# Moving a pair's weighted rows one slot later on VectorE, between the next pair's two small weight operations, in a two-layer graph attention kernel

## The chip, the cores and the metric

The kernel runs on one core of a Trainium2 chip (trn2). The time is device microseconds (us) from start to end of one execution on that core. The kernel before takes 2144.38 us, the median of three runs (2143.71 to 2145.70).

## The reference

6250 nodes with 768 features are normalised and rectified, sent through two graph attention layers (4 heads of 64, then 1 head of 256) and two dense layers, and added to the input. There are 100000 edges, sorted by destination, and a self loop for each node. What bears on the change is the attention layer:

```python
def gat_conv(x, src, dst, W, a_src, a_dst, bias, heads):
    h = (x @ W).reshape(n, heads, -1)
    alpha_s = (h * a_src[None]).sum(-1)
    alpha_d = (h * a_dst[None]).sum(-1)
    e = leaky_relu(alpha_s[src] + alpha_d[dst], 0.2)
    e = exp(e - segment_max(e, dst)[dst])
    alpha = e / (segment_sum(e, dst)[dst] + 1e-16)
    out = segment_sum(h[src] * alpha[:, :, None], dst)
    return out.reshape(n, -1) + bias
...
h = maximum(layernorm(x), 0)
h = relu(gat_conv(h, src, dst, W1, a_src1, a_dst1, b1, 4))
h = relu(gat_conv(h, src, dst, W2, a_src2, a_dst2, b2, 1))
return x + relu(h @ Wm1 + bm1) @ Wm2 + bm2
```

## The kernel before

**Stages.** First, node features, scores and a table of rows in device memory are made, a tile of 128 nodes at a time. Then `layer_edges` (L530) runs for layer 1 and again for layer 2. Between the edges of a layer, a `Node` object turns finished sums into the next table (layer 1, L778) or into the output (layer 2, L878).

**Tiling.** Edges go in tiles of 128, a *pair* is two tiles, a *group* is two pairs (`TPG = 4`). There are 196 groups; 782 tiles hold edges, so a layer has 391 pairs. The order is written out by hand (`manual_schedule`, L304): each engine works through its own instructions in the order in which the Python code issues them. The loop over groups is at L708.

**One pair.** For every tile, `gather` (L545) issues one indirect DMA from GpSimd (POOL) that fetches 128 table rows into `G` (L554). Then `pair` (L612) does the following:

- ScalarE takes two exponentials of the gathered scores, `e1` (L619) and `e2` (L621).
- VectorE multiplies `v = e2 * rho` (L624) and takes `w = max(v, e1)` (L634 in layer 1, L627 in layer 2). These are the two small weight operations. `rho`, `v`, and in layer 1 also `w`, lie in `e_ps` in PSUM.
- VectorE makes the weighted rows `hw`. In layer 1 this is one multiplication of the gathered rows by `w` (L636); in layer 2 it is two tensor-scalar instructions that write a weighted one-hot matrix from `iota_ps` (L631).
- TensorE adds two products to the sums `o_ps` (L648). Layer 1 multiplies the one-hot tile `hot` (L582) with `hw`; layer 2 multiplies `hw` with `G`.

So the last reader of `G` is VectorE in layer 1 and TensorE in layer 2.

**Around it.** Two pairs stand in each group. Between them come `advance` (steps of the node work), `make_hot(g + 1)`, every fourth group `meet(t + 1)` (16 small matmuls, L600, that spread the destinations' `rho`), and every other group `make_mask`. Behind the second pair come `join` (L608), and in every odd group `gather_up` (L659), which adds up `o_ps` on VectorE (`acc`, L669) and copies parts of it on ScalarE (`sum`, L678). The first tiles of each layer are fetched before the table is complete (L300) and put right in `first_whole` (L275).

**Buffers.** `G` comes from a pool of twenty pairs, which both layers share, and the gathers of group g + 8 stand ahead of pair (g, 0):

```python
gp = ...tile_pool(name="gathered", bufs=2 * (AHEAD + 2))   # AHEAD = 8
...
gather(g + AHEAD)
pair(g, 0)
```

Of the kernel before, what the change touches and what calls it, by code (L numbers as in the profile page):

```python
# [30 lines left out]
NG = NQ  # L31
# [22 lines left out]
def kernel(  # L54
# [21 lines left out]
    nc = tc.nc  # L76
# [440 lines left out]
    def fetch_rows(r):  # L517

        if r < NET // 16:
            drow[r] = rowsp.tile([P, 16 * P], BF16, name="drow")  # L520
            nc.sync.dma_start(drow[r], bcast(dmod_d, 16 * P, r * 16 * P))
# [8 lines left out]
    def layer_edges(layer, H, node, pre, matched, pre_pool):  # L530
# [4 lines left out]
        with tc.tile_pool(name=f"eg{layer}", bufs=5) as eg, \  # L535
                tc.tile_pool(name=f"hw{layer}", bufs=10 if layer == 1 else 14) as hwp, \
                tc.tile_pool(name=f"sum{layer}", bufs=4) as sums, \
                tc.tile_pool(name=f"sm{layer}", bufs=4) as sm:
            G, hot, e_ps, o_ps = {}, {}, {}, {}

            def tiles(g):

                return range(max(TPG * g, FIRST) - TPG * g, min(TPG * g + TPG, LAST) - TPG * g)

            def gather(g):  # L545
                if not 0 <= g < NG:
                    return
                for t in tiles(g):
                    k = TPG * g + t
                    if k // 2 not in G:  # L550
                        G[k // 2] = first_G[layer].get(k // 2) or rows_in(layer)
                    if k < FIRST + len(THERE[layer]):
                        continue
                    nc.gpsimd.indirect_dma_start(  # L554
                        out=G[k // 2][:, k % 2], out_offset=None, in_=table[layer],
                        in_offset=bass.IndirectOffsetOnAxis(ap=src_i[:, k:k + 1], axis=0))
# [18 lines left out]
            def make_hot(g):  # L575

                if layer == 2 or not 0 <= g < NG:
                    return
                T = tiles(g)
                k, n = TPG * g + T[0], len(T)  # L580
                hot[g] = eg.tile([P, TPG, P], F32, name="hot")
                nc.vector.tensor_tensor(  # L582
                    hot[g][:, T[0]:T[0] + n], iota_ps.unsqueeze(1).to_broadcast([P, n, P]),
                    dcol[:, k:k + n].unsqueeze(2).to_broadcast([P, n, P]), ALU.is_equal)
# [27 lines left out]
            def pair(g, p):  # L612

                if 2 * p not in tiles(g):
                    return
                Gp = G.pop(TPG // 2 * g + p)
                sc = Gp[:, :, RW[1]:] if layer == 1 else Gp[:, :, HID:HID + 1]
                e1 = sm.tile([P, 2, H], F32, name="e1")
                nc.scalar.activation(e1, sc, AF.Exp)  # L619
                e2 = sm.tile([P, 2, H], F32, name="e2")  # L620
                nc.scalar.activation(e2, sc, AF.Exp, scale=SLOPE)  # L621
                at = TPG * (g % 4) + 2 * p
                rho, v, w = (e_ps[g // 4][:, at:at + 2, k * H:(k + 1) * H] for k in range(3, 6))
                nc.vector.tensor_mul(v, e2, rho)  # L624
                if layer == 2:
                    w = sm.tile([P, 2, H], F32, name="w")
                    nc.vector.tensor_max(w, v, e1)  # L627
                    hw = hwp.tile([P, 2, P], F32, name="hw")
                    for t in range(2):
                        k = TPG * g + 2 * p + t  # L630
                        nc.vector.tensor_scalar(hw[:, t], iota_ps, dcol[:, k:k + 1], w[:, t],  # L631
                                                ALU.is_equal, ALU.mult)
                else:
                    nc.vector.tensor_max(w, v, e1)  # L634
                    hw = hwp.tile([P, 2, H, C + 1], F32, name="hw")
                    nc.vector.tensor_mul(  # L636
                        hw, Gp[:, :, :RW[1]].rearrange("p t (h c) -> p t h c", h=H),
                        w.unsqueeze(3).to_broadcast([P, 2, H, C + 1]))
                u = g // 2
                if u not in o_ps:  # L640
                    o_ps[u] = ps.tile([P, RW[layer]], F32, name="o_ps", tag="o", bufs=3)
                for t in range(2):
                    k = 2 * p + t
                    if layer == 2:
                        l, r = hw[:, t], Gp[:, t]
                    else:
                        l, r = hot[g][:, k], hw[:, t].rearrange("p h c -> p (h c)")
                    nc.tensor.matmul(o_ps[u], l, r[:, :RW[layer]], start=(g % 2 == 0 and k == 0),  # L648
                                     stop=(g % 2 == 1 and k == tiles(g)[-1]))

            def stay_warm(n):

                if layer == 1:
                    for _ in range(n):
                        nc.tensor.matmul(idle_ps[0], idle[:, :P], idle, start=True, stop=True)
# [3 lines left out]
            def gather_up(u):  # L659

                if u == NU - 1:

                    late.append(node.steps(NT - 1, None, run[0], o_ps.pop(u)))
                    return
                acc = sums.tile([P, RW[layer]], F32, name="acc")
                if u == 0:
                    nc.vector.tensor_copy(acc, o_ps.pop(u))
                else:
                    nc.vector.scalar_tensor_tensor(acc, run[0], keep[:, u % 2:u % 2 + 1],  # L669
                                                   o_ps.pop(u), ALU.mult, ALU.add)  # L670
                for Q in (2 * u - 1, 2 * u):
                    t, q = divmod(Q, 4)
                    if not 0 <= t < NT - 1:
                        continue
                    if q == 0:
                        done[t] = sums.tile([P, RW[layer]], F32, name="sum", bufs=3)
                    r = slice(32 * q, 32 * q + 32)
                    nc.scalar.activation(done[t][r], acc[r], AF.Copy)  # L678
                    if q == 3:
                        late.append(node.steps(t, done.pop(t)))  # L680
                if u == NU - 2:
                    nc.vector.memset(acc[96:], 0.0)
                    run[0] = node.whole(NT - 1, acc)
                else:
                    run[0] = acc

            def advance(g):

                for _ in range(2 if NG - 4 <= g < NG - 2 else 1):
                    for step in list(late):  # L690
                        if next(step, 0) == 0:
                            late.remove(step)
# [15 lines left out]
            for g in range(NG):  # L708
                t, j = divmod(g, 4)
                if g == NG - 2:  # L710
                    at_end.append(g)
                gather(g + AHEAD)
                pair(g, 0)
                if g == NG - 1:
                    pair(g, 1)
                if g == NG - 2:
                    gather_up(NU - 2)
                advance(g)
                if g <= NG - 4:
                    make_hot(g + 1)  # L720
                if g in (NG - 4, NG - 3):
                    make_hot(g + 2)
                if j == 0:
                    if layer == 1:
                        fetch_rows(t + 4)
                    node.prefetch(t)
                    meet(t + 1)
                elif j == (2 if t < NT - 1 else 1):
                    node.ahead(t)
                elif j % 2:  # L730
                    make_mask((g + 7) // 2)
                if g == NG - 3:
                    idle_ps.append(ps.tile([P, 4 * P], F32, name="idle_ps", tag="e"))
                if g >= NG - 3:
                    stay_warm(3)
                if g < NG - 1:
                    pair(g, 1)
                advance(g)
                if j == 3:
                    join(t + 1)  # L740
                if g % 2 and 5 <= g < NG - 6:
                    gather_up((g - 5) // 2)
                elif g in (NG - 6, NG - 5, NG - 3):
                    gather_up({NG - 6: NU - 5, NG - 5: NU - 4, NG - 3: NU - 3}[g])
                if NG - 3 <= g < NG - 1:
                    stay_warm(3)
                hot.pop(g, None)
                if layer == 1 and g == NG - 6:
                    first_sources(2)
            gather_up(NU - 1)  # L750
# [22 lines left out]
    with tc.tile_pool(name="w2p", bufs=1) as wp, tc.tile_pool(name="wk2", bufs=2) as wk:  # L773
# [48 lines left out]
        with tc.tile_pool(name="pre1", bufs=1) as pre:  # L822
            first_hits(pre, 1, 0)
            pre1 = prepare(pre, 1, 4)
            layer_edges(1, 4, Node1(), pre1,
                        lambda: scores_in(ps, w2, *w2_in, KH, 1), pre)
# [428 lines left out]
```

## Time and profile before

| what | value |
|---|---|
| time, median of 3 runs | 2144.38 us (2143.71 to 2145.70) |
| profiled execution: its own time, its span | 2556.39 us, 2554.4 us |
| mean granted TensorE clock in it | 0.760 |
| busy: PE, DVE, POOL, ACT | 1572.4, 1325.8, 1599.2, 545.2 us |
| gathers L554 on POOL | 1545, 951 ns each |
| v L624, w L634, hw L636 in layer 1 | 391 each; 166, 174, 695 ns |
| v L624, w L627 in layer 2 | 391 each; 157, 159 ns |
| hw L631 in layer 2 | two per pair, 406 ns recorded |

The profiled execution is 412 us longer than the median. Its timeline is therefore read for durations and for distances between instructions in undisturbed stretches, and not for the total of its idle times. In a timeline line the columns are: start in us, length in us, engine, line of the source, operation, output and inputs, count, and in brackets the idle time before it and what ended that. PE is TensorE's matmul, PEld its weight load, DVE VectorE, ACT ScalarE, POOL GpSimd, SP the engine whose queue issues plain DMAs.

### The profile page before, as it was taken

The page shows a single profiled execution, that of the slowest core. Times are in us where ns is not written, and L with a number is a line of the kernel's source. Part 1 is how long each engine was busy: PE and PEld are TensorE (multiplying, and loading weights), DVE is VectorE, ACT ScalarE, POOL GpSimd, SP SyncE. Part 2 cuts the span into 40 slices and gives each one's busy share as a digit, 9 for nine tenths or more (in the row PEclk, how much of TensorE's full clock was granted, in tenths as well). Part 3 has the DMA queues.
Part 4 walks back from the last instruction along what each step waited for, and adds up shares of the span by engine and source line. Part 5 has one row for each costly group of instructions (what it writes and reads, how often), then busy time and mean ns, then how long its engine had stood idle before and what let it go on. Part 6 is the DMA issues. An engine that isn't in the chain of part 4 may idle for free.

```text
span 2554.4 us, 26518 instructions
## 1 busy us (share of the span) xinstructions
PE 1572.4 (62%) x6764; PEld 1116.8 (44%) x6765; DVE 1325.8 (52%) x4164; ACT 545.2 (21%) x2601; POOL 1599.2 (63%) x1759
## 2 busy tenths in 40 slices
PE   9963455545554556546554557666676676666667
PEld 7852334433433334324342444444454444444444
DVE  7844555555655556546562444444444444444444
ACT  4630111111121111112121112222222222222212
POOL 6875666666666666666635566666666666666661
PEclk9986677667777777777776777777877787778789
DMA  9954454445454454444434444544554455445442
GB/s 353 344 164 145 128 148 138 132 138 150 135 147 140 136 149 141 137 136 146 138 91 134 125 134 130 152 149 136 155 151 144 142 153 152 144 144 153 147 150 66
DMA packets 157543, 383.12 MB, mean 150 GB/s; under 512 B 35543, under 2 KB 50222, under 8 KB 157382
## 3 DMA queue, kind: packets, MB, share of 16 engines
q0 software_dynamic: 75072, 209.10, 30.4%
q1 hardware_dynamic: 80940, 170.75, 19.1%
q10 hardware_dynamic: 1370, 1.48, 0.2%
q8 instruction: 58, 0.95, 0.1%
q14 instruction: 103, 0.84, 0.1%
HBM read 323.07 MB, written 58.13 MB: 149 GB/s over the span
## 4 chain that ended last, share of the span: by engine, by line
DVE 18%; another core or an unknown queue 15%; PE 14%; issue 13%; ACT 3%; DMA 0%; POOL 0%; ACTq 0%; DVEq 0%; POOLq 0%
PE o_ps L648 8%; DVE hw L631 6%; DVE hw L636 3%; PE y_ps L939 3%; DVE e_ps L624 2%; DVE w L627 1%; PE tp L923 1%; ACT sum L678 1%; DVE acc L669 1%; DVE y L942 1%; DVE e_ps L634 1%; PE e_ps L600 1%; DVE hot L582 1%; PE y_ps L875 0%
## 5 line engine op out<-in xcount | busy, mean ns | idle before, releaser
L554 POOL DMA_INDIRECT G<-table,src_i x1545 | 1469.0, 951 | 822.9 <-issue 535.8
L648 PE MATMUL o_ps<-hw,hot 128*128 128x260 f32 x1564 | 541.4, 482 | 316.2 <-issue 204.4
L648 PEld LDWEIGHTS o_ps<-hw,hot 128*128 128x128 f32 x1564 | 344.8, 235 | 482.5 <-issue 278.6
L648 PE MATMUL o_ps<-G,hw 128*128 128x258 f32 x1564 | 488.2, 460 | 61.3 <-issue 41.2
L648 PEld LDWEIGHTS o_ps<-G,hw 128*128 128x128 f32 x1564 | 352.8, 233 | 168.7 <-issue 59.6
L624 DVE TENSOR_TENSOR e_ps<-e,e_ps 128x8 f32<-128x8 f32 (+1 forms) x782 | 126.5, 162 | 515.7 <-ACT e L621 172.4
L678 ACT ACTIVATE sum<-acc 32x260 f32<-32x260 f32 (+1 forms) x384 | 159.9, 416 | 991.4 <-DVE acc L669 730.4
L600 PE MATMUL e_ps<-win,mask 128*128 128x12 bf16 (+1 forms) x1564 | 88.2, 169 | 372.7 <-issue 356.5
L636 DVE TENSOR_TENSOR hw<-G,e_ps 128x520 f32<-128x520 f32 x391 | 271.9, 695 | 76.9 <-DVE e_ps L634 46.3
L631 DVE TENSOR_SCALAR hw<-iota_ps,dcol,w 128x128 f32<-128x128 f32 x782 | 285.0, 406 | 17.7 <-DVE w L627 2.9
L600 PEld LDWEIGHTS <-mask 128*128 128x128 bf16 x1564 | 75.2, 103 | 393.5 <-issue 369.3
L942 DVE TENSOR_TENSOR y<-y_ps,xt 128x384 f32<-128x384 f32 (+1 forms) x98 | 54.0, 552 | 233.5 <-remote 209.6
L619 ACT ACTIVATE e<-G 128x8 f32<-128x8 f32 (+1 forms) x782 | 151.4, 195 | 110.5 <-issue 57.7
L939 PE MATMUL y_ps<-wm,mT 128*128 128x384 f32 x392 | 160.9, 535 | 11.1 <-issue 7.5
L582 DVE TENSOR_TENSOR hot<-iota_ps,dcol 128x512 f32<-128x512 f32 x196 | 133.5, 681 | 34.1 <-remote 34.1
L621 ACT ACTIVATE e<-G 128x8 f32<-128x8 f32 (+1 forms) x782 | 149.4, 192 | 0.0
L350 PE MATMUL h_ps<-w,r 128*128 128x256 f32 x588 | 135.0, 384 | 4.4 <-ACT r L341 4.4
L923 PE MATMUL tp<-rT,wm 128*128 128x128 f32 x392 | 68.0, 328 | 111.4 <-issue 81.9
L634 DVE TENSOR_TENSOR e_ps<-e_ps,e 128x8 f32<-128x8 f32 x391 | 68.1, 174 | 131.5 <-remote 96.4
L769 ACT ACTIVATE rT<-tp,bT 128x128 f32<-128x128 f32 x196 | 60.7, 362 | 293.5 <-remote 243.3
L350 PEld LDWEIGHTS h_ps<-w,r 128*128 128x128 f32 x588 | 109.7, 193 | 22.6 <-ACT r L341 5.7
L923 PEld LDWEIGHTS tp<-rT,wm 128*128 128x128 f32 x392 | 59.8, 229 | 125.6 <-issue 91.1
(405 smaller groups left out, 1201.3 us busy)
## 6 DMA issues: line engine op xcount, KB each, us to landing
xt<-in_x SPq DMA_DIRECT2D x96, 384.0 KB
drow<-dmod_d SPq DMA_DIRECT2D x49, 512.0 KB
mask_d<-mask SPq DMA_DIRECT2D x97, 256.0 KB
mask<-mask_d SPq DMA_DIRECT2D x97, 256.0 KB
G<-table,src_i POOLq DMA_INDIRECT x1545
xTt<-in_xT SPq DMA_DIRECT2D x49, 384.0 KB
out<-y SPq DMA_DIRECT2D x48, 384.0 KB
table<-kept SPq DMA_DIRECT2D x49, 132.0 KB
```

The costliest lines, as they stand in the source:

```text
L350: nc.tensor.matmul(h_ps, r[:, k], w1[:, k], start=(k == 0), stop=(k == KI - 1))
L554: nc.gpsimd.indirect_dma_start(out=G[k // 2][:, k % 2], out_offset=None, in_=table[layer], in_offset=bass.IndirectOffsetOnAxis(ap=src_i[:, ...
L582: nc.vector.tensor_tensor(hot[g][:, T[0]:T[0] + n], iota_ps.unsqueeze(1).to_broadcast([P, n, P]), dcol[:, k:k + n].unsqueeze(2).to_broadca ...
L600: nc.tensor.matmul(e_ps[t][:, at + k, :3 * H], m[:, k * P:(k + 1) * P], pre.win[:, 2 * u + 2], start=True, stop=True)
L619: nc.scalar.activation(e1, sc, AF.Exp)
L624: nc.vector.tensor_mul(v, e2, rho)
L631: nc.vector.tensor_scalar(hw[:, t], iota_ps, dcol[:, k:k + 1], w[:, t], ALU.is_equal, ALU.mult)
L636: nc.vector.tensor_mul(hw, Gp[:, :, :RW[1]].rearrange("p t (h c) -> p t h c", h=H), w.unsqueeze(3).to_broadcast([P, 2, H, C + 1]))
L648: nc.tensor.matmul(o_ps[u], l, r[:, :RW[layer]], start=(g % 2 == 0 and k == 0), stop=(g % 2 == 1 and k == tiles(g)[-1]))
L678: nc.scalar.activation(done[t][r], acc[r], AF.Copy)
L923: nc.tensor.matmul(m_ps[:, j], wm1[:, k, j * P:(j + 1) * P], rT[:, k], start=(k == 0), stop=(k == KH - 1))
L939: nc.tensor.matmul(y_ps, mT[:, j], wm2[:, j, s * half:(s + 1) * half], start=False, stop=(j == KH - 1))
```

## The change

In `pair`, what follows the two small operations is split off into `onto_sums`: the `hw` instructions and the two products into `o_ps`. `pair` now issues `v` of its own pair, then `onto_sums` of the pair before, then its own `w`, and leaves its own pair in the list `weighed` for the next call. In the last two groups (`g >= NG - 2`) a pair's `onto_sums` follows at once. Nothing is computed that wasn't, and no buffer count is altered. In the changed kernel `hw` is at L644 (layer 1) and L640 (layer 2), `w` at L629, the products at L656; `v` stays at L624.

```diff
-            G, hot, e_ps, o_ps = {}, {}, {}, {}
+            G, hot, e_ps, o_ps, weighed = {}, {}, {}, {}, []
...
                 nc.vector.tensor_mul(v, e2, rho)
+                while weighed:
+                    onto_sums(*weighed.pop())
                 if layer == 2:
                     w = sm.tile([P, 2, H], F32, name="w")
-                    nc.vector.tensor_max(w, v, e1)
+                nc.vector.tensor_max(w, v, e1)
+                weighed.append((g, p, Gp, w))
+                if g >= NG - 2:
+                    onto_sums(*weighed.pop())
+
+            def onto_sums(g, p, Gp, w):
+
+                if layer == 2:
                     hw = hwp.tile([P, 2, P], F32, name="hw")
                     for t in range(2):
                         k = TPG * g + 2 * p + t
                         nc.vector.tensor_scalar(hw[:, t], iota_ps, dcol[:, k:k + 1], w[:, t],
                                                 ALU.is_equal, ALU.mult)
                 else:
-                    nc.vector.tensor_max(w, v, e1)
                     hw = hwp.tile([P, 2, H, C + 1], F32, name="hw")
                     nc.vector.tensor_mul(
                         hw, Gp[:, :, :RW[1]].rearrange("p t (h c) -> p t h c", h=H),
...
-                hot.pop(g, None)
+                hot.pop(g - 1, None)
```

## The prediction, made before the changed kernel had run

> **What bounds the kernel now.** I read the page's busy shares and cost groups first, then the timeline of GpSimd alone, then all engines in an undisturbed stretch, and last the starts of the two layers.
>
> ```profile
> PE 1572.4 (62%) x6764; PEld 1116.8 (44%) x6765; DVE 1325.8 (52%) x4164; ACT 545.2 (21%) x2601; POOL 1599.2 (63%) x1759
> ...
> L554 POOL DMA_INDIRECT G<-table,src_i x1545 | 1469.0, 951 | 822.9 <-issue 535.8
> ...
> L636 DVE TENSOR_TENSOR hw<-G,e_ps 128x520 f32<-128x520 f32 x391 | 271.9, 695 | 76.9 <-DVE e_ps L634 46.3
> L631 DVE TENSOR_SCALAR hw<-iota_ps,dcol,w 128x128 f32<-128x128 f32 x782 | 285.0, 406 | 17.7 <-DVE w L627 2.9
> ```
>
> No engine is above 63%, so shares do not name the bound. But a gather never follows the last without a gap. In the timeline, around two gathers of layer 1:
>
> ```profile
> 1009.03 0.17 DVE L624 TENSOR_TENSOR e_ps<-e,e_ps 128x8 f32<-128x8 f32 x1
> 1009.24 0.17 DVE L634 TENSOR_TENSOR e_ps<-e_ps,e 128x8 f32<-128x8 f32 x1
> 1009.35 0.95 POOL L554 DMA_INDIRECT G<-table,src_i  x1 [0.30 <-issue]
> 1009.44 0.69 DVE L636 TENSOR_TENSOR hw<-G,e_ps 128x520 f32<-128x520 f32 x1
> 1010.06 0.68 DVE L582 TENSOR_TENSOR hot<-iota_ps,dcol 128x512 f32<-128x512 f32 x1
> 1010.60 0.95 POOL L554 DMA_INDIRECT G<-table,src_i  x1 [0.31 <-issue]
> ```
>
> 0.95 plus 0.30 us: GpSimd takes a gather every 1.25 us when nothing stops it. Now add that up for the unprofiled run. The first early gather (L300) starts at 146.25 and the first L554 of layer 1 at 157.48. 774 gathers of layer 1 x 1.25 = 967.5, which gives 1125.0; layer 2 has 11 + 771 = 782, x 1.25 = 977.5, which gives 2102.5. The median is 2144.4, so 41.9 us remain. Of these 2.0 lie around the span (2556.39 - 2554.4) and 20.7 are the end of layer 2 (last e2, L621, starts at 2533.70; the span ends at 2554.4). That leaves **19.2 us** for the switch between layers, two landings and every stall of GpSimd. The kernel is paced by gathers from end to end. The 412 us that the profiled execution is longer are mostly stalls of its own: GpSimd's last gather of layer 1 starts at 1313.12 in it, where 157.48 + 773 x 1.25 is 1123.7.
>
> The others keep up. `acc` (L669) comes once in two groups; in layer 1 it starts at 1302.28, 1309.88, 1319.09 and 1326.29, so two groups cost 24.0 / 3 = 8.0 us of the slowest engine's time, against 8 x 1.25 = 10.0 for their gathers. In layer 2 neighbouring `acc`s stand 6.9 apart (1720.16, 1727.03).
>
> The exception is the start of a layer, where GpSimd fills its twenty pairs and then waits for pair 0 to let go of its rows:
>
> ```profile
> 196.44 0.95 POOL L554 DMA_INDIRECT G<-table,src_i  x1 [0.30 <-issue]
> 206.37 0.17 DVE L624 TENSOR_TENSOR e_ps<-e,e_ps 128x8 f32<-128x8 f32 x1
> 206.57 0.17 DVE L634 TENSOR_TENSOR e_ps<-e_ps,e 128x8 f32<-128x8 f32 x1
> 206.78 0.69 DVE L636 TENSOR_TENSOR hw<-G,e_ps 128x520 f32<-128x520 f32 x1
> 207.40 0.68 DVE L582 TENSOR_TENSOR hot<-iota_ps,dcol 128x512 f32<-128x512 f32 x1
> 208.00 0.16 DVE L624 TENSOR_TENSOR e_ps<-e,e_ps 128x8 f32<-128x8 f32 x1
> 208.22 0.95 POOL L554 DMA_INDIRECT G<-table,src_i  x1 [10.84 <-issue]
> ...
> 1402.90 0.95 POOL L554 DMA_INDIRECT G<-table,src_i  x1 [0.30 <-issue]
> 1419.31 0.94 POOL L554 DMA_INDIRECT G<-table,src_i  x1 [15.46 <-ACT e L619]
> ```
>
> The reader is to see that the gather at 208.22 follows the end of pair 0's `hw` (207.47). The label "issue" means that no releaser was seen. By the 19.2 us, at most part of these 10.5 and 15.2 us (less the usual 0.30) is in the unprofiled run.
>
> **What the Trainium skill says.** "DMA: Bandwidth & Descriptors", section "SWDGE vs HWDGE vs iDMA": a DMA issued from GpSimd, an indirect one too, has its descriptors computed in software there. The steady 0.95 us of L554 agrees. "SBUF — State Buffer", section "Who interferes with whom": GpSimd is shut out of a port pair that it shares with VectorE while VectorE runs in a two-port mode, and with its reads while a VectorE instruction has two SBUF inputs. Here `hw` takes `e_ps` or `iota_ps` from PSUM, and the gather at 1009.35 keeps its 0.95 us beside L636; the change alters no operand's place, so I take no effect from it. "VectorE: DVE Perf Modes", section "The DRAIN you can't avoid": a semaphore between VectorE operations costs nothing extra. The trace differs for small ones: `v` to the dependent `w` is 0.20 us from start to start, while the copy L155 at 205.84 is followed by the independent L608 after 0.07. I use the trace.
>
> **The change, part by part.**
> *VectorE's order.* Nothing is removed: 391 pairs a layer keep one `v`, one `w` and their `hw`. Before, layer 1 has two dependent steps per pair: 0.21 (`v` to `w`), 0.20 (`w` to `hw`), then 0.62 to what follows: 1.03. After, `v`, `hw` of the pair before, `w`: in layer 1 `hw` still carries a wait on VectorE itself (it reads the PSUM tile that `v` writes), so 0.20; `hw` to `w` 0.62; `w` to an independent successor about 0.08, an estimate from L155's 0.07. Sum 0.90, saving 0.13. In layer 2 before: 0.19 + 0.19 + 0.65 = 1.03; after, `hw` has no such wait: 0.08 + 0.65 + 0.20 (the next `v` waits for `w`) = 0.93, saving 0.10. In all 391 x 0.13 + 391 x 0.10 = **90 us of VectorE time**. From both sides: 0 if every step stays held, 391 x 2 x 2 x 0.12 = 188 if none is. On the path it counts 0, because 8.0 us of work already hide behind 10.0 us of gathers. If that cover were gone, it would be a gain.
> *The wait that `hw` inherits.* It now stands behind `v` of the next pair, which waits for that pair's e2 and so for its gather to land. Behind it on VectorE are `w`, `make_hot`, `acc`; TensorE's products wait for it. In the steady state this is one pair's gathers, 2.5 us, of delay in a pipeline that has twenty pairs: 50 us. `gather_up` at the end of odd group g reads sums whose last pair is of group g - 4, so it waits for nothing new. Cost 0.
> *Release of `G`.* One slot later. It counts only where GpSimd stands at the end of its buffers, that is at pair 0. Layer 1: `hw` of pair 0 moves from 206.78 behind `hot` and `v` of pair 1: 206.78 + 0.62 + 0.20 = 207.60, **+0.8 us**. Layer 2: there is no `hot`; `hw` moves behind one `v`, +0.1 to +0.2, and the products behind `meet(1)`, whose 16 matmuls take 0.54 us (L600 at 1418.40) and can run before `hw` is there: **+0.2**, at most +0.7. If the stall at the start is not in the unprofiled run, each is 0.
> *Ends.* In group NG - 2 VectorE does two `hw` in one slot (+0.7 us), and `acc` of `gather_up(NU - 2)` waits for products issued just ahead of it, about +0.3. Three pairs at 2.5 us each follow, in which VectorE needs 1.03: gone before the last landing. 0, at most +0.8 per layer.
> *Queues.* No DMA is moved. GpSimd's and SP's instructions keep their order; ScalarE's too.
> Sum: 0 + 0 + 0.8 + 0.2 + 0 = +1.0, halved for the chance that the stalls are absent: +0.5. Against the profiled execution's 2556.39 it is the same +0.5, and that execution has stalls that move far more; against the median it gives 2144.9.
>
> **Rivals.**
> *Compute sets part of the pace (faster).* For it: GpSimd waited 129.0 us for ScalarE's L928 and 59.8 for L769 in the profile. Against it: the 19.2 us. That is the ceiling; half of it gives 2144.4 - 9.6 = 2134.8.
> *Late release at a full pool (slower).* If GpSimd meets the end of its buffers more often than at two starts, each meeting costs one slot of layer 1, about 1.7 us (206.37 to 208.00). For it: in the profile it does so often. Against it: the 19.2 us allow few. It decides from the third meeting on (3 x 1.7 = 5.1); five give +8.5, 2152.9. `hw` held behind a `v` that waits for ScalarE adds up to 1.25 us where `sum` (L678) stands ahead of `e1`, which belongs to the same case.
> *The change does not do what it says.* The changed kernel's instruction order has `v`, `hw`, `w` in both layers, so this is excluded.
>
> **How the numbers follow.** What a measurement of this kernel can tell from no change is 0.2%, 4.3 us. No effect on the path: 0.74, at 2144.9, own range 2143 to 2148. Late release: 0.17. Compute pace: 0.09. The range reaches into both, 2137 to 2154, and leaves out the far halves of the two rivals.
>
> **What would show it.** In the changed profile: gathers still 0.95 + 0.30; `v` to `hw` to `w` as 0.2 (layer 1) or 0.08 (layer 2) and 0.62 to 0.65; idle before L629 near zero; pair 0's `hw` one slot later in layer 1. GpSimd stalls more often in undisturbed stretches, or a gather interval other than 1.25, would prove me wrong; so would a time below 2140 or above 2149.

## The result: 6 us slower, and the profile after

The changed kernel takes **2152.34 us** (median of 7 runs, 2147.24 to 2153.69) against 2145.70 us for the kernel before (7 runs beside it, 2143.55 to 2149.14). The ratio is 1.0028 [1.0016, 1.0040], or +6.0 us [3.4, 8.6]. That is slower by more than the 0.2% that was set as the measurable bound. It lies inside the predicted range, but outside the 2143 to 2148 of the likeliest case, and above the 2149 that the prediction had named as a sign of being wrong.

Some chips grant TensorE a mean clock of about 0.76 and run the kernels of this document in 2550 to 2595 us, with or without a profile, others grant 0.82 to 0.84 and run them in 2143 to 2155. The profile before came from the first kind and the profile after from the second, so idle times of the two pages are not compared as an effect of the change; distances between a few instructions are.

The page of the changed kernel, shares of the engines and cost groups (columns as before: busy time, mean ns of one, idle time before it and its main releaser):

```profile
PE 1577.6 (73%) x6762; PEld 1088.8 (51%) x6765; DVE 1263.3 (59%) x4164; ACT 598.4 (28%) x2601; POOL 1603.2 (75%) x1759
...
L554 POOL DMA_INDIRECT G<-table,src_i x1545 | 1472.9, 953 | 470.8 <-issue 256.3
...
L624 DVE TENSOR_TENSOR e_ps<-e,e_ps 128x8 f32<-128x8 f32 (+1 forms) x782 | 129.7, 166 | 789.5 <-ACT e L621 780.0
...
L619 ACT ACTIVATE e<-G 128x8 f32<-128x8 f32 (+1 forms) x782 | 160.3, 205 | 1104.4 <-DMA G<-table,src_i 1066.6
...
L640 DVE TENSOR_SCALAR hw<-iota_ps,dcol,w 128x128 f32<-128x128 f32 x782 | 282.5, 402 | 0.1
L644 DVE TENSOR_TENSOR hw<-G,e_ps 128x520 f32<-128x520 f32 x391 | 271.9, 695 | 12.5 <-DVE e_ps L624 0.9
```

Three things are to be seen. A gather still costs 0.95 us and the two forms of `hw` take as long as before (695 and 402 ns, against 695 and 406). VectorE is 62.5 us less busy than in the page before (1263.3 against 1325.8). And VectorE has time to spare: ahead of `v` (L624) it stands idle 789.5 us, waiting for ScalarE's second exponential, which in turn follows L619, and L619 waits 1066.6 us for landings. In such a stretch a saving on VectorE only makes that wait longer.

GpSimd's own waits (engine, line, releaser: total us, times, longest us) show the pace. The longest waits ahead of L554 are:

```profile
POOL G L554 <- issue: 256.3, 841, 0.4
POOL G L554 <- PE o_ps L656: 54.5, 179, 0.3
```

No wait ahead of an L554 is longer than 0.4 us, from the first to the last. GpSimd never stood at the end of its twenty pairs in this execution.

**The new order, layer 1 and layer 2.** From the timeline of the changed kernel, one pair each:

```profile
1113.86 0.17 DVE L624 TENSOR_TENSOR e_ps<-e,e_ps 128x8 f32<-128x8 f32 x1 [3.49 <-ACT e L621]
1114.06 0.69 DVE L644 TENSOR_TENSOR hw<-G,e_ps 128x520 f32<-128x520 f32 x1
...
1114.79 0.17 DVE L629 TENSOR_TENSOR e_ps<-e_ps,e 128x8 f32<-128x8 f32 x1
...
1114.87 0.42 DVE L801 TENSOR_TENSOR all__10258<-mine,sum 128x260 f32<-128x260 f32 x1
...
2105.74 0.17 DVE L624 TENSOR_TENSOR e_ps<-e,e_ps 128x2 f32<-128x2 f32 x1 [1.16 <-ACT e L621]
2105.81 0.73 DVE L640 TENSOR_SCALAR hw<-iota_ps,dcol,w 128x128 f32<-128x128 f32 x2
...
2106.45 0.15 DVE L629 TENSOR_TENSOR w<-e_ps,e 128x2 f32<-128x2 f32 x1
2106.52 0.20 DVE L608 TENSOR_REDUCE e_ps<-e_ps 128x14 f32<-128x42 f32 x1
```

In layer 2 the small steps have shrunk: 0.07 from `v` to `hw`, 0.64 to `w`, 0.07 to what follows. In layer 1 they have not: 0.20, then 0.73, then 0.08. But every eighth pair of layer 1, the first one of a group g that is a multiple of four, goes differently:

```profile
1123.99 0.17 DVE L624 TENSOR_TENSOR e_ps<-e,e_ps 128x8 f32<-128x8 f32 x1 [1.11 <-ACT e L621]
...
1124.07 0.70 DVE L644 TENSOR_TENSOR hw<-G,e_ps 128x520 f32<-128x520 f32 x1
...
1124.68 0.17 DVE L629 TENSOR_TENSOR e_ps<-e_ps,e 128x8 f32<-128x8 f32 x1
```

Here it is 0.08 and 0.61. Of the 373 pairs of layer 1 from 205 to 1135 us whose three instructions stand directly behind each other, these are 47, each eighth one, and the other 326 have 0.72 to 0.74 from `hw` to `w`. The code shows what sets them apart: `e_ps` is one tile for every four groups, so in these pairs the `hw`, which is that of the pair before, reads `w` from another `e_ps` than the one that `v` and `w` are written to. In the other pairs it is the same tile, and each step costs 0.12 us more.

**Where the time went.** NG is the number of groups, 196, and NU is half of it, the number of `gather_up` calls in a layer. The end of layer 2 in the changed kernel: the first `v` below belongs to pair (NG-2, 0), the first pair of the group before the last; the `acc` in the last line is the one of `gather_up(NU - 2)`, which is called straight behind that pair:

```profile
2120.03 0.95 POOL L554 DMA_INDIRECT G<-table,src_i  x1 [0.30 <-issue]
...
2121.80 1.56 PE L947 MATMUL y_ps<-wm,mT 128*128 128x384 f32 x4
2121.88 0.17 DVE L624 TENSOR_TENSOR e_ps<-e,e_ps 128x2 f32<-128x2 f32 x1 [1.23 <-ACT e L621]
2121.95 0.72 DVE L640 TENSOR_SCALAR hw<-iota_ps,dcol,w 128x128 f32<-128x128 f32 x2
...
2123.55 1.56 PE L947 MATMUL y_ps<-wm,mT 128*128 128x384 f32 x4
2124.62 1.82 PEld L656 LDWEIGHTS o_ps<-G,hw 128*128 128x128 f32 x8
2124.94 1.90 PE L656 MATMUL o_ps<-G,hw 128*128 128x258 f32 x8
2126.01 0.48 DVE L677 SCALAR_TENSOR_TENSOR acc<-acc,keep,o_ps 128x258 f32<-128x258 f32 x1 [2.51 <-PE o_ps L656]
```

And the same place in the kernel before (the run before_again, on a 0.76 chip; first line the products of pair (NG-3, 1)):

```profile
2540.92 1.04 PE L648 MATMUL o_ps<-G,hw 128*128 128x258 f32 x4
...
2542.15 1.56 PE L939 MATMUL y_ps<-wm,mT 128*128 128x384 f32 x4
2542.98 0.17 DVE L624 TENSOR_TENSOR e_ps<-e,e_ps 128x2 f32<-128x2 f32 x1 [2.67 <-ACT e L621]
2543.90 1.56 PE L939 MATMUL y_ps<-wm,mT 128*128 128x384 f32 x4
2544.02 0.47 DVE L669 SCALAR_TENSOR_TENSOR acc<-acc,keep,o_ps 128x258 f32<-128x258 f32 x1
```

Before, the products of the last pair that this `acc` sums stand *ahead* of the two sets of output matmuls (L939, node work that `advance(NG - 3)` issues), and `acc` starts without a wait, 1.04 us behind `v`. After, they are issued in the next pair's slot, so they stand *behind* both sets (L947) in TensorE's order: `acc` waits 2.51 us and starts 4.13 us behind `v`. That is **+3.1 us**. The eight matmuls of L656 in that line are the products of two pairs, and `acc` needs the first four.

TensorE doesn't take the products first, though `hw` for them is done by about 2122.7 (L640, 2121.95 + 0.72). This fits what the Trainium skill says in "Perfetto Trace Analysis", section "Tensor Engine Instruction (MATMUL, LD_WEIGHTS)": TensorE's queue has only a limited reorder, which can pull a weight load ahead of matmuls in flight. The trace agrees: the weight load L656 starts at 2124.62, inside the L947 that runs to 2125.11; the matmuls come at about its end (2124.94; ends of matmuls are modelled).

The chain of work that ended last in the changed kernel (start, us, engine, output, line) runs through this order:

```profile
2119.88 1.72 PE o_ps L656 x4
2121.60 0.26 PE y_ps L883
2121.87 1.49 PE y_ps L947 x4
2123.35 0.26 PE y_ps L883
2123.62 1.49 PE y_ps L947 x4
2125.10 0.88 PE o_ps L656 x4
...
2126.01 0.49 DVE acc L677
```

The two sets of node work, with their first matmuls (L883), hold 3.5 us of it. Not all of the +3.1 us is theirs: `hw` of pair (NG-3, 1) now stands behind this `v` on VectorE too. Had its four matmuls followed `hw` at once, `acc` could have started at about 2123.75 (an estimate: 2122.67, 1.04 for the four, and 0.04 to `acc`), 0.8 us later than before; the other 2.3 us are the node work in front.

Layer 1 has the same knot, with `h_ps` (L822) and the matmuls of `stay_warm` (L663, whose result nobody reads) in front:

```profile
1132.59 0.17 DVE L624 TENSOR_TENSOR e_ps<-e,e_ps 128x8 f32<-128x8 f32 x1 [1.24 <-ACT e L621]
...
1133.85 1.03 PE L822 MATMUL h_ps<-w,rT 128*128 128x258 f32 x4
...
1134.73 0.81 PE L663 MATMUL idle_ps<-idle 128*128 128x512 bf16 x3
...
1135.37 1.92 PE L656 MATMUL o_ps<-hw,hot 128*128 128x260 f32 x8
1136.45 0.48 DVE L677 SCALAR_TENSOR_TENSOR acc<-acc,keep,o_ps 128x260 f32<-128x260 f32 x1 [2.02 <-PE o_ps L656]
...
1141.32 0.95 POOL L300 DMA_INDIRECT G<-table,first_i  x1 [6.81 <-DMA table<-kept]
```

`v` to `acc` is 3.86 us here. In four executions of the kernel before it was 1.83, 2.17, 2.94 and 3.00, so this end costs **0.9 to 2.0 us** in this execution, 1.7 against the 2.17. Behind `acc` comes the chain to the next layer: `sum`, `kept` (L825), the store of the table, and then GpSimd's first gather of layer 2 at 1141.32.

Together 4.8 us (3.09 + 1.69) of the 6.0 measured. Two things make this sum rough. The distances of the kernel before are from chips at 0.76. And `v` itself comes a little earlier in the changed order: from `v` of pair (NG-4, 0) to the `acc` of `gather_up(NU - 3)` it is 6.75 us in layer 2 of before_again and 6.16 in after_again (both runs stand below), and 7.16 and 6.87 in layer 1, all at 0.76. Less these 0.6 and 0.3 us, about 3.9 us remain (an estimate). The rest lies within the interval, which begins at 3.4.

### The profile page after: what moved, and what is told of

Its sections match the earlier page's. It is cut to its first block, busy times and chain, and to the rows that moved or that the text cites. A ratio compares the mean times of both kernels' runs of the same rounds, so it can differ in the third digit from the quotient of the medians.

```text
span 2150.5 us, 26808 instructions
## 1 busy us (share of the span) xinstructions
PE 1577.6 (73%) x6762; PEld 1088.8 (51%) x6765; DVE 1263.3 (59%) x4164; ACT 598.4 (28%) x2601; POOL 1603.2 (75%) x1759
## 4 chain that ended last, share of the span: by engine, by line
DMA 33%; PE 30%; DVE 19%; issue 7%; POOL 5%; ACT 5%; ACTq 0%; DVEq 0%; POOLq 0%
DMA G<-table,src_i 33%; PE o_ps L656 13%; PE y_ps L947 7%; DVE hw L644 6%; POOL G L554 5%; PE h_ps L350 5%; DVE e_ps L624 2%; ACT e L619 2%; DVE hot L582 2%; DVE hw L640 1%; PE tp L931 1%; DVE e_ps L629 1%; ACT sum L686 1%; PE y_ps L883 1%; ACT e L621 1%
## 5 line engine op out<-in xcount | busy, mean ns | idle before, releaser
L554 POOL DMA_INDIRECT G<-table,src_i x1545 | 1472.9, 953 | 470.8 <-issue 256.3
L656 PE MATMUL o_ps<-hw,hot 128*128 128x260 f32 x1564 | 573.1, 516 | 304.6 <-DVE hw L644 301.7
L656 PE MATMUL o_ps<-G,hw 128*128 128x258 f32 x1564 | 468.6, 437 | 234.4 <-DVE hw L640 233.6
L656 PEld LDWEIGHTS o_ps<-hw,hot 128*128 128x128 f32 x1564 | 363.5, 251 | 475.3 <-DVE hw L644 413.7
L624 DVE TENSOR_TENSOR e_ps<-e,e_ps 128x8 f32<-128x8 f32 (+1 forms) x782 | 129.7, 166 | 789.5 <-ACT e L621 780.0
L656 PEld LDWEIGHTS o_ps<-G,hw 128*128 128x128 f32 x1564 | 316.9, 215 | 357.7 <-DVE hw L640 287.5
L619 ACT ACTIVATE e<-G 128x8 f32<-128x8 f32 (+1 forms) x782 | 160.3, 205 | 1104.4 <-DMA G<-table,src_i 1066.6
L640 DVE TENSOR_SCALAR hw<-iota_ps,dcol,w 128x128 f32<-128x128 f32 x782 | 282.5, 402 | 0.1
L644 DVE TENSOR_TENSOR hw<-G,e_ps 128x520 f32<-128x520 f32 x391 | 271.9, 695 | 12.5 <-DVE e_ps L624 0.9
L947 PE MATMUL y_ps<-wm,mT 128*128 128x384 f32 x392 | 202.9, 653 | 0.7 <-ACT mT L936 0.7
L621 ACT ACTIVATE e<-G 128x8 f32<-128x8 f32 (+1 forms) x782 | 148.7, 190 | 0.6
L947 PEld LDWEIGHTS y_ps<-wm,mT 128*128 128x128 f32 x392 | 87.5, 247 | 68.1 <-issue 41.5
L677 DVE SCALAR_TENSOR_TENSOR acc<-acc,keep,o_ps 128x260 f32<-128x260 f32 (+1 forms) x192 | 90.9, 473 | 4.5 <-PE o_ps L656 4.5
L629 DVE TENSOR_TENSOR e_ps<-e_ps,e 128x8 f32<-128x8 f32 x391 | 67.7, 173 | 11.7
L365 POOL TENSOR_TENSOR ha<-kept,a1b 128x512 f32<-128x512 f32 x45 | 53.3, 1184 | 25.7 <-ACT kept L356 25.6
L600 PEld LDWEIGHTS <-mask 128*128 128x128 bf16 x1564 | 57.4, 100 | 16.6 <-issue 9.9
```

The lines of the kernel that those rows point to most:

```text
L554: nc.gpsimd.indirect_dma_start(out=G[k // 2][:, k % 2], out_offset=None, in_=table[layer], in_offset=bass.IndirectOffsetOnAxis(ap=src_i[:, ...
L644: nc.vector.tensor_mul(hw, Gp[:, :, :RW[1]].rearrange("p t (h c) -> p t h c", h=H), w.unsqueeze(3).to_broadcast([P, 2, H, C + 1]))
L947: nc.tensor.matmul(y_ps, mT[:, j], wm2[:, j, s * half:(s + 1) * half], start=False, stop=(j == KH - 1))
```

## The experiments

Two theories went in. **Theory 1**: the cost sits at the ends of the two layers, where a pair's products now follow node work in TensorE's order. **Theory 2**: the cost is spread over the 391 pairs of a layer, by `G`, `hot` and `o_ps` being let go later. The measure beside the time is the distance from `v` of pair (NG-2, 0) to the next `acc`. It suits the purpose because what follows it is alike in all kernels looked at, whatever their order: from that `acc` to the end of the span 24.1 to 25.8 us, in layer 1 from `acc` to the first L300 4.8 to 5.2 us.

At 0.76 something else than at 0.83 paces the kernel. In the profile before, TensorE stands idle ahead of the products for 245.6 us in which the profile shows no releaser. The others wait for it: around 1573 to 1587 us ScalarE waits 16.56 us for products and VectorE 14.25 us for ScalarE. GpSimd meanwhile runs far ahead, and is through with layer 1 some 40 us before layer 2 can begin:

```profile
PE o_ps L648 <- issue: 245.6, 184, 3.4
...
1354.06 0.95 POOL L300 DMA_INDIRECT G<-table,first_i  x1 [40.00 <-DVE e_ps L634]
```

The idle time ahead of L554 is 822.9 us there, and 470.8 in the changed kernel at 0.83, which is little more than 1545 times the usual 0.30. At 0.76 GpSimd's gathers do not set the pace, and the last gather starts 53 us ahead of the end of the span, not 30.5. So the first three sets show what the order does at the ends, and in a loop that TensorE's waits hold up; the loop that is paced by gathers stands in the fourth.

### First set, on a chip with the clock at 0.76 (kernel before 2562.38 us)

**before_again** is the kernel before, unaltered, to see its ends beside those of the other kernels.

> The kernel before, profiled once more, for a timeline of its two layer ends that is as undisturbed as that of the kernel after. Theory 1 (the whole cost lies at the two layer ends, where the products of the last delayed pair stand in TensorE's queue behind work of the nodes): from v of pair (NG-2, 0) to the acc of gather_up(NU-2) some 2.2 us in layer 1 and 1.0 us in layer 2, against 3.9 and 4.1 in the kernel after; gathers 0.95 + 0.30 us without longer stalls inside a layer. Theory 2 (the cost is spread over the layers, through later release of the gathered rows): GpSimd's gathers of one layer take less time from first to last than in the kernel after, by some 3 us per layer.

Measured: 2570.62 us, clock 0.757. `v` to `acc` is 1.04 us in layer 2, as expected, and 3.00 in layer 1, where 2.2 was expected.

**flush_one_group_earlier** ends the delay one group sooner. The products of pair (NG-3, 1) are then ahead of the node work again, and 386 of 391 pairs per layer are still delayed.

```diff
-                if g >= NG - 2:
+                if g >= NG - 3:
```

> The kernel after, but the delay ends one group earlier (g >= NG - 3), so that no pair whose sums gather_up(NU-2) reads is carried over into group NG-2. Theory 1: the cost goes, 2145 to 2147 us, ratio to before 0.999 to 1.001. Theory 2: nearly all pairs are still delayed, so the cost stays, ratio 1.002 to 1.004, about 2151 us.

Measured: 2563.06 us, ratio 1.0004 [0.9993, 1.0016]. `v` to `acc` is 1.04 in layer 2 and 1.32 in layer 1. The delay of nearly all pairs, without the knot at the end, costs nothing that can be seen at this clock.

**delay_at_end_only** is the reverse: only groups NG-4 and NG-3, four pairs of 391 per layer, are delayed; all others have the old order.

```diff
-                if g >= NG - 2:
+                if g >= NG - 2 or g < NG - 4:
```

> Only the pairs of groups NG-4 and NG-3 are delayed; all earlier pairs keep the order of the kernel before. Theory 1: the whole cost is there, ratio 1.0015 to 1.0035, about 2150 us. Theory 2: four of 391 pairs are delayed, ratio 1.000, about 2146 us.

Measured: 2565.85 us, ratio 1.0018 [1.0007, 1.0029], or +4.6 us. `v` to `acc` is 3.39 in layer 2 and 3.86 in layer 1. Four pairs are enough for a slowdown.

**delay_layer1_only** leaves layer 2 in the old order.

```diff
-                if g >= NG - 2:
+                if layer == 2 or g >= NG - 2:
```

> The delay only in layer 1; layer 2 has the order of the kernel before. Theory 1: by the timelines 1.7 of 4.8 us belong to the end of layer 1, so about +2 us, ratio 1.0005 to 1.0015. Theory 2: half of the cost, ratio 1.001 to 1.002, or all of it where the release by VectorE in layer 1 is what counts.

Measured: 2563.97 us, ratio 1.0010 [0.9998, 1.0023]. `v` to `acc` is 1.04 in layer 2, as before, and 4.83 in layer 1. The distances answer to the layer that was altered; the time (-0.5 to +5.9 us) is inconclusive, since both theories allow it.

### Second set, on another chip at 0.76 (kernel before 2578.11 us)

**before_third** is again the kernel before.

> The kernel before once more, profiled beside the three that follow. Theory 1 (cost at the two layer ends): v of pair (NG-2, 0) to the acc of gather_up(NU-2) in layer 2 takes 1.0 us again, and from the start of the last gather to the end of the span about 3 us less than in the kernel after; from the last gather of layer 1 to the first early gather of layer 2 about 1.7 us less. Theory 2 (cost spread over the layers): these distances are equal and the gathers of a layer take longer in the kernel after.

Measured: 2577.66 us; 1.04 in layer 2, 2.94 in layer 1. The expected distance from the last gather to the end of the span, 3 us shorter than in the changed kernel, did not come: it is 52.5 us here and 50.2 in after_again, on the same chip. With GpSimd that far ahead, the last gather is no mark for the end.

**after_again** is the changed kernel, unaltered.

> The kernel after on the same chip as the other kernels of this call. Both theories: ratio 1.0016 to 1.004.

Measured: 2585.47 us, ratio 1.0040 [1.0021, 1.0059]. `v` to `acc` is 3.40 and 5.22. From `v` of pair (NG-2, 0) in layer 2 to the end of the span it takes 29.17 us, where before_third takes 25.10 and flush_again 26.42.

**flush_again** is flush_one_group_earlier once more, beside the changed kernel.

> The delay ends one group earlier (g >= NG - 3), on the same chip as the kernel after. Theory 1: ratio to before 0.999 to 1.0005, and the acc of gather_up(NU-2) 1.0 us behind v in layer 2. Theory 2: the ratio of the kernel after, 1.002 to 1.004.

Measured: 2579.45 us, ratio 1.0014 [1.0000, 1.0029]; 1.04 and 1.51. VectorE's waits that end with products of TensorE for an `acc`, in after_again and in flush_again (total us, times, longest):

```profile
DVE acc L677 <- PE o_ps L656: 5.1, 2, 3.4
```

```profile
DVE acc L677 <- PE o_ps L656: 0.4, 1, 0.4
```

The two long waits, one per layer, are gone with one group's earlier end. On time alone this run left a remainder of +0.14%, with an interval that begins at zero, so it was run once more below.

**one_more_copy_per_pair** asks whether VectorE's time is covered, as both the prediction and Theory 1 hold. It is the kernel before with a copy of no use ahead of each pair's `v`.

```diff
+                pad = sm.tile([P, P], F32, name="pad")
+                nc.vector.tensor_copy(pad, iota_ps)
```

> The kernel before with one added VectorE copy of 128 x 128 from PSUM in every pair, whose result nobody reads: 782 x about 0.26 us, some 200 us of VectorE time. If gathers pace the kernel and VectorE's time is covered: where the gathers run without longer stalls, +0 to +3 us (the ends of the layers only), ratio 1.000 to 1.0015. If VectorE's time lies on the path: up to +9%, and then the time that the new order saves on VectorE should have been a gain.

The copies in its groups:

```profile
L625 DVE COPY pad<-iota_ps 128x128 f32<-128x128 f32 x782 | 220.4, 282 | 0.0
```

Measured: 2570.47 us, ratio 0.9975 [0.9958, 0.9992]. 220 us more on VectorE did not make the kernel slower. That it became 0.25% *faster* was expected by neither theory, and no run here tells why. The run speaks for chips at 0.76 only; one at 0.83 was not tried.

### Third set, at 0.76 (kernel before 2562.18 us)

**before_fourth**: the kernel before, on a chip that again grants 0.76, so the numbers that were expected for the higher clock are not comparable.

> The kernel before, profiled once more, in the hope of a chip whose granted TensorE clock is the 0.83 of the profile of after. Theory 1 (cost at the two layer ends) then: last gather of layer 1 to first early gather of layer 2 some 6 us, where the kernel after has 7.8; start of the last gather to the end of the span 27 to 28 us, where it has 30.5; gathers of a layer equally long in both, within 1 us.

Measured: 2566.05 us; 1.05 in layer 2, 1.83 in layer 1.

**flush_third**: the earlier end of the delay for the third time.

> The delay ends one group earlier (g >= NG - 3). Theory 1: ratio to before 0.9995 to 1.0005; if the granted clock is 0.83, 2144 to 2147 us. Theory 2: 1.002 to 1.004.

Measured: 2562.89 us, ratio 1.0001 [0.9990, 1.0012]; 1.04 and 1.03. Of the three ratios, 1.0004, 1.0014 and 1.0001, two have intervals around 1 and the third begins at it.

### Fourth set, on a chip at 0.82 to 0.83 (kernel before 2148.10 us)

Here the two kernels that decide stand on the kind of chip that the prediction was about.

**after_third** is the changed kernel; **delay_at_end_again** is delay_at_end_only, four pairs per layer.

> The kernel after, beside the one that delays only the pairs of groups NG-4 and NG-3. Theory 1 (all cost at the two ends): both have the same ratio to before, 1.0018 to 1.003. Theory 2 (some of the cost spread over the layers): this one is slower than the other by more than 0.1%.

> Only the pairs of groups NG-4 and NG-3 are delayed. Theory 1: ratio 1.0018 to 1.003, as the kernel after of this call. Theory 2: 1.000 to 1.001, and the kernel after above it.

Measured: after_third 2152.16 us, ratio 1.0023 [1.0013, 1.0033]; delay_at_end_again 2152.10 us, ratio 1.0021 [1.0012, 1.0030]. `v` to `acc` is 3.39 and 3.83 in the first, 3.49 and 4.75 in the second. `v` and `acc` at the end of layer 2 in delay_at_end_again:

```profile
2121.00 0.17 DVE L624 TENSOR_TENSOR e_ps<-e,e_ps 128x2 f32<-128x2 f32 x1 [1.60 <-ACT e L621]
...
2124.49 0.48 DVE L677 SCALAR_TENSOR_TENSOR acc<-acc,keep,o_ps 128x258 f32<-128x258 f32 x1 [1.86 <-PE o_ps L656]
```

and its waits of the same kind:

```profile
DVE acc L677 <- PE o_ps L656: 4.8, 2, 2.9
```

**Verdict.** By their ratios, four delayed pairs per layer cost +4.5 us and all 388 cost +4.9 us; by the medians +4.0 and +4.1, and the two kernels differ by 0.06 us. What the 384 other pairs' new order gives or takes is therefore zero, within about 0.1%. Theory 1 is shown, for the place and for the size; Theory 2 falls. That an end of the delay one group sooner takes the cost away is shown at 0.76 alone; at the higher clock flush_one_group_earlier was not run. How the sum divides between the two layers is less sure: in layer 2 all runs agree (+2.3 to +3.1), in layer 1 the distance varies from run to run in the kernel before (1.83 to 3.00) and with the delay (3.83 to 5.22), and no profile of the kernel before at the higher clock was to be had. So it is open too whether that kernel also has the 6.08 us landing of the gather of 2110.03, through which the chain that ended last runs just before the end of layer 2. delay_at_end_again has a similar one there (5.28 us), so the new order in the loop is not what makes it.

## Why the prediction was right about the loop and wrong about the ends

**The range: held by luck.** The forecast was +0.5 us, with 2144.9 as the likeliest time; measured are +6.0 us and 2152.34. The range reaches so far only because its upper part was laid for the late release of `G`, and that did not happen.

**The pace: right.** Gathers stay at 0.95 + 0.30 us, and no wait ahead of L554 exceeds 0.4 us. For stalls there was even less room than the 19.2 us: in layer 1 the 773 steps from the first L554 (157.30) to the last (1133.57) take 976.3 us instead of 966.3, with no wait above 0.4 us, because single gathers run longer than 0.95 us. Only the reason given for the 412 us longer profiled execution was wrong: the prediction called them mostly stalls of the profile's own, but kernels on chips at 0.76 take 2550 to 2595 us without a profile too.

**VectorE's order, 90 us saved and 0 on the path: right on the path, off in the parts.** In layer 2 the pair takes 0.07 + 0.64 + 0.07 = 0.78 where 0.93 was expected, because what follows `w` there is independent of it, not the next `v`. In layer 1 it takes 0.20 + 0.73 + 0.08 = 1.01 where 0.90 was expected, against 1.03 before. The term mis-sized is "`hw` to `w` 0.62": 0.62 is what an independent instruction takes behind `hw`, and this `w` came only after 0.73 in seven pairs of eight. It is not held by reading what `v` wrote: the `w` of layer 2 reads that too and comes after 0.64, and so does the `w` of every eighth pair of layer 1, after 0.61. What the slow pairs share is that `hw` reads the very `e_ps` tile that `w` is written to. So layer 1 saves almost nothing and layer 2 more than twice its part; that the sum, about 117 us (an estimate: 391 x 0.25, and 391 x 0.05 with every eighth pair at 0.77), is not far from the 90 is the two errors working against each other. That the time is covered is shown at 0.83 by four delayed pairs and 388 costing the same, and at 0.76 by 220 us of extra copies that did not slow the kernel.

**The wait that `hw` inherits, 0 in the steady state: right**, and the sentence in support of it, that `gather_up` reads sums of group g - 4, holds there. It does not hold for `gather_up(NU - 2)`, whose last pair is the one directly before.

**Release of `G`, +0.8 and +0.2 if the stall exists: it doesn't** at this clock, so both are 0. With that the rival "late release at a full pool" falls, although its 2152.9 is near the measured time (by its own lines the slot is 208.00 - 206.37 = 1.63 us and not 1.7, which gives 2152.5). The mechanism was another.

**Ends, "0, at most +0.8 per layer": this is the step that failed.** The prediction found the right instruction, the `acc` of `gather_up(NU - 2)`, and charged it with +0.7 for a second `hw` and "about +0.3" for products issued just ahead of it. The first is near what the trace gives (0.8 of the +3.1 above). But it looked at VectorE and left out what else is in TensorE's order by then: the node work of `advance(NG - 3)`, some 2.3 us. Measured from `v` to `acc`: +3.1 us in layer 2 (+2.3 to +3.1 in all runs with the delay) and +0.9 to +2.0 in layer 1. The second half of the step, that three pairs at 2.5 us follow and the loss is gone before the last landing, is refuted by one line: the last gather starts at 2120.03, and with the page's median of 3.0 us to landing it is there by about 2123.0; `acc` comes at 2126.01. From the last gather to the end of the span 30.5 us remain (2150.5 - 2120.03), and in them the chain that ended last holds node work, products and `acc`, and no gather. A delay in that chain has no cover.

**Queues: right.** Nothing moved on GpSimd's, SP's or ScalarE's. The point that counted was TensorE's order, which the prediction went through for `meet(1)` at a layer's start and not for the end.

**"Compute sets part of the pace" (faster): fell.** No run of the changed kernel, or of a part of the change, was faster.

## What to carry to other kernels

Work that is issued one slot later is judged twice: in the loop, where a full pipeline hid it here, and at the drain (the end of a layer, where no new pairs come in), where nothing did. At the drain, write out the order of every in-order engine between the delayed producer and its first reader, and price what now stands in front. Here moving the flush, the point from which pairs are no longer delayed, one group forward left the rest of the loop as it was and took the cost away (1.0001 to 1.0014, on chips at 0.76), but a version that beats the kernel before wasn't found, since the VectorE time that is saved was covered from the start.

## What the runs showed of the hardware beyond this

- The granted TensorE clock differs between chips far more than the change is worth: the same kernel takes 2562 to 2578 us at a mean of 0.76 and 2146 to 2148 us at 0.82 to 0.83, a fifth more, though its bound at the higher clock is GpSimd's gathers. At 0.76 TensorE has 245.6 us of waits ahead of the products without a releaser that the profile shows (L648 in the profile before); at 0.83 the list of waits has none of that kind for the products' matmuls. What makes them was not looked into.
- A VectorE operation that writes the PSUM tile which the `hw` just ahead (0.69 us) reads starts 0.73 us behind it, and one that writes another tile after 0.61; a `hw` that reads the tile which the `v` just ahead writes starts after 0.20, otherwise after 0.08. Every eighth pair of layer 1 shows it within one execution. So sharing a tile with the neighbour costs 0.12 us a step here; no run gave the neighbours tiles of their own.
- One copy of 282 ns per pair, on a path with much idle VectorE time, went with a time 0.25% shorter on a chip at 0.76. The cause is open.
